# An RWKV block on one core: the recurrence per batch on lanes of a head and a quarter of its key channels

## The chip, the core and the metric

The kernel runs on one core of a Trainium2 chip. The metric is the device time of one execution in microseconds (us), and it is given as the median of several runs. Everything is fp32. A core has a matrix engine (TensorE, PE in the profile, with its weight loads as PEld), a vector engine (VectorE, DVE), a scalar engine (ScalarE, ACT), a general engine (GpSimd, POOL) and a sync engine (SyncE, SP) that here only issues DMAs. Each engine runs its own instructions strictly in the order in which the program gives them; semaphores order them between engines. SBUF is the on-chip memory of 128 partitions, PSUM the accumulator memory of the matrix engine.

## The reference

There are 32 batches of 128 steps with 512 channels; 32 heads of 16 channels. A layer norm, a token shift and five mixes give the inputs of five projections. Then each head runs a recurrence over the 128 steps with a 16 x 16 state, and a group norm, a gate and two more matrix products follow. Cut to what matters:

```python
xn = _ln(x, ln1_w, ln1_b); sx = _token_shift(xn, state[:, 1])
xxx = tanh((xn + sx * maa_x) @ maa_w1) ... @ maa_w2
x5 = xn[:, :, None] + sx[:, :, None] * (maa_stack + xxx)
w = exp(-exp(time_decay + tanh(x5[:, :, 1] @ decay_w1) @ decay_w2))
r, k, v = x5[..3] @ Wr.T, x5[..0] @ Wk.T, x5[..2] @ Wv.T ; g = silu(x5[..4] @ Wg.T)
def step(s, (r_t, k_t, v_t, w_t)):            # per batch and head, s is 16 x 16
    a = k_t[:, :, :, None] * v_t[:, :, None, :]
    out = einsum('bhk,bhkd->bhd', r_t, u * a + s)
    return (a + w_t[:, :, :, None] * s, out)
att = group_norm(outs) * gn_w + gn_b
x = x + att * g @ Wo.T
xn2 = _ln(x, ln2_w, ln2_b); sx2 = _token_shift(xn2, state[:, 0])
x = x + sigmoid(xr @ ffn_Wr.T) * (square(relu(xk @ ffn_Wk.T)) @ ffn_Wv.T)
```

## The kernel before, in words

**Groups.** The 32 batches go in 8 groups of 4 (`GB`, `NG`), so that a group is 512 columns in the channel layout (128 partitions of channels, four chunks e of them, batch and step along the row). For each group a front (layer norm, mixes, projections: `front_mix`, `front_proj`, `front_gate`), a recurrence (`rec_*`) and a back (`back`) are made. The last group's back is made in two halves of two batches.

**Order.** Nothing is scheduled by the chip. `Plan.run` (lines 147 to 190) keeps a model of the five engines, the buffers and one DMA queue. Every step of the work is an `Op` with an engine and an estimated time. Among the steps that can start about first, the one with the earliest due time (`DUE`) is issued next, and so one fixed order of instructions for each engine comes out, written once.

**Projections.** `matmuls` (line 392) gives four matmuls of 128 x 128 by 512 columns for each output chunk; in the trace each fp32 matmul is two instructions. Two narrower forms put two matmuls side by side in the array: `first_split` (line 398, 64 or 32 output columns each, two column tiles) and `side_by_side` (line 411, 64 rows each, two row tiles).

**Into lanes.** The recurrence works on lanes: one partition for a (batch, head) pair, 4 x 32 = 128 of them, and all 16 key channels along the row. `to_lanes` (lines 414 to 421) copies each output chunk of w, k, v and r from the channel layout to lanes by four DMAs from SBUF to SBUF, two issued by SP and two by ACT, in runs of 512 bytes. That is 64 DMAs for a group.

**Preparation.** Two steps are folded into one, so that the scan runs over 64 pairs. `prep` (line 569) multiplies k at even steps by w at odd ones, r at odd steps by w at even ones (lines 604, 606), and makes the product of decays w01 (line 625). `bonus` (line 632) sums r·k·u over the 16 key channels (lines 635 to 643, one instruction per key channel) and r·k of neighbouring steps (lines 648 to 655). All this runs on VectorE in the lane layout.

**Recurrence.** One unit is (key channel q, half dh of the 8 value channels): 32 units for a group, 256 in all. ACT writes the decays into PSUM (line 680) and the first state (line 691); POOL multiplies k by v (line 705) and adds the pairs (line 709); VectorE scans (line 727) and multiplies by r (line 729) into `rm`. TensorE then sums over q: `rec_pe` (line 762) transposes `rm` against a permuted identity, accumulating in PSUM, 8 transposes for each unit, and 8 more for a 17th unit that VectorE makes for the bonus (lines 736 to 743). ACT copies the sum from PSUM to `y` (line 776).

**Back.** Group norm (lines 804 to 819), transposes back into the channel layout (line 830), scaling, the gate from DRAM (line 834), then Wo (line 850), layer norm, and the feed-forward part (lines 392, 924, 940), and the output.

Of the kernel before, what the change touches and what calls it, by code (L numbers as in the profile page):

```python
# [14 lines left out]
P = 128  # L15
B, L, E = 32, 128, 512
H, S = 32, 16
NE = E // P
HE = P // S
GB = 4  # L20
NG = B // GB
# [4 lines left out]
NU = NDH * (S + 1)  # L26
# [19 lines left out]
EPSILON = 0.0457  # L46


DUE = {"rec": (0.169, 1.075), "mix": (-5.141, -3.246), "proj": (-5.191, 5.259), "gate": (0.565, 0.599), "prep": (-4.508, 1.678), "back": (0.059, 3.118), "last1": (-21.936, 10.98), "warm0": (-5.0, -3.0), "warm1": (5.624, 7.819), "last2": (6.858, 12.052)}
# [23 lines left out]
class Plan:  # L73
# [12 lines left out]
    def add(self, gen, v0, v1, steps):  # L86

        st = [gen, None, 0, v0, (v1 - v0) / steps]
        self.streams.append(st)
        self.advance(st, None)  # L90
# [92 lines left out]
def rwkv6_block(ctx: ExitStack, tc: tile.TileContext, x, prev, s0, vecs, u, maa_w1, maa_w2,  # L183
                decay_w1, decay_w2, wr, wk, wv, wg, wo, fk, fr, fv, out):

# [8 lines left out]
    def tag(pool, shape, name, bufs):  # L203
        def make():
# [8 lines left out]
        (big, [P, S, L], "w", 1), (big, [P, S, L], "r", 2), (big, [P, S, L], "k", 2), (big, [P, S, L], "v", 2),  # L213
        (big, [P, GB * H, S], "y", 1),
        (big, [P, S, T2], "w01", 1), (big, [P, S, S], "st", 2), (big, [P, L], "rk", 2), (big, [P, T2], "a10", 2),
        (big, [P, DH, L], "am", 1), (big, [P, DH, T2], "a", 2), (big, [P, DH, L], "rm", 2),
# [3 lines left out]
        (ps, [P, N], "ps", 4), (ps, [P, DH, T2], "sc", 2), (ps, [P, DH, P], "acc", 1),  # L220
    ]
    plan = Plan({name: tag(pool, shape, name, bufs) for pool, shape, name, bufs in spec})

# [4 lines left out]
    u_sb = const.tile([P, S], F32, name="u_sb")  # L228

# [8 lines left out]
    by_head = const.tile([P, P], F32, name="by_head")  # L240
    make_identity(nc, ident)
    nc.gpsimd.tensor_copy(by_head.rearrange("p (b e h) -> p b e h", b=GB, e=NE),
                          ident.rearrange("p (b h e) -> p b e h", b=GB, e=NE))
    nc.gpsimd.memset(mhalf, -0.5)
    nc.gpsimd.memset(thb.t, 0.0)
    nc.vector.memset(w2p, 0.0)

    def constants():
# [18 lines left out]
        for e in range(NE):  # L267
            nc.sync.dma_start(out=lanes(u_sb, e), in_=u[e * HE : (e + 1) * HE, :].unsqueeze(0).to_broadcast([GB, HE, S]))

    def lanes(t, e):  # L270


        return t[e::NE]
# [10 lines left out]
    def load_x(g, need=None, bs=range(GB)):  # L284
        b0, b1 = bs[0], bs[-1] + 1
        (xt,) = yield Op(SP, 0.4, w=[(0, None)], alloc=["x"], xfer=part(4.5, bs), need=need)
        nc.sync.dma_start(out=xt[:, b0:b1, :], in_=x[g * GB + b0 : g * GB + b1].rearrange("b t e -> t b e"))
        return xt
# [8 lines left out]
    def center(w):  # L297


# [14 lines left out]
        centered.append(dw)  # L314

    def part(us, bs):

        return us if len(bs) == GB else us * len(bs) / GB + 0.03

    def layernorm_T(g, src, sums, vw, vb, which, use, take, need=None, bs=range(GB)):  # L320

        b0, nb_ = bs[0], len(bs)
        bsl, cols = slice(b0, b0 + nb_), slice(b0 * L, (b0 + nb_) * L)
        if sums is None:
            xh = src
            stats, mv = yield Op(DVE, 0.88, r=[(src, b0)], w=[(0, b0), (1, b0)], alloc=["stats", "mv"])
            for b in bs:  # L330
                if b != b0:
                    yield Op(DVE, 0.88, r=[(src, b)], w=[(stats, b), (mv, b)])
                nc.vector.bn_stats(stats[:, b, :], src[:, b, :])
                nc.vector.bn_aggr(mv[:, b, :], stats[:, b, :])
# [21 lines left out]
        for b in bs:  # L356
# [6 lines left out]
                       pv[:, 1 - which, :, g * GB + b0 : g * GB + b0 + nb_])  # L363
        late = []

        def evict(e, pt):
            yield Op(ACT, part(0.78, bs), r=[(pt, None)], w=[(xnT, e)])
            nc.scalar.activation(xnT[:, e * GB + b0 : e * GB + b0 + nb_, 1 : L + 1], bt(pt[:, cols]), AF.Identity,
                                 bias=col(vb, e), scale=col(vw, e))
            yield from use(xnT, e, pt, tiles)  # L370
# [15 lines left out]
    def row(xnT, e, shift, bs=range(GB)):  # L386

        return xnT[:, e * GB + bs[0] : e * GB + bs[-1] + 1, shift : shift + L]

    def matmuls(p, w, xin, e, cols=slice(0, N)):  # L390
        for c in range(NE):
            nc.tensor.matmul(p, lhsT=w[:, c, e * P : (e + 1) * P], rhs=xin[:, c, cols], start=(c == 0), stop=(c == NE - 1))  # L392

    def first_split(p, w, rows, xin):

        for c in range(NE):
            for h in range(2):
                nc.tensor.matmul(p[h * XD : h * XD + rows, 0 : N // 2], lhsT=w[:, c, :],  # L398
                                 rhs=xin[:, c, h * N // 2 : (h + 1) * N // 2], start=(c == 0), stop=(c == NE - 1))

    def in_both_halves(t, p, rows):

        for h in range(2):
            for k in range(2):
                nc.scalar.activation(t[k * XD : k * XD + rows, h * N // 2 : (h + 1) * N // 2],
                                     p[h * XD : h * XD + rows, 0 : N // 2], AF.Tanh)

    def side_by_side(pp, w, up, low):

        for p, h, t in zip(pp, (slice(0, XD), slice(XD, P)), (up, low)):  # L410
            nc.tensor.matmul(p.t, lhsT=w[h, :], rhs=t[h, :], start=True, stop=True)  # L411

    def to_lanes(d, name, src, e):

        for eng, queue, bs, end in ((SP, nc.sync, (0, 1), []), (ACT, nc.scalar, (2, 3), [src])):
            if name not in d:
                (d[name],) = yield Op(eng, 1.32, r=[(src, None)], w=[(0, (e, eng))], alloc=[name], xfer=1.2, end=end)
            else:
                yield Op(eng, 1.32, r=[(src, None)], w=[(d[name], (e, eng))], xfer=1.2, end=end)
            for b in bs:  # L420
                queue.dma_start(out=lanes(d[name].t[b * H : (b + 1) * H], e), in_=src[:, b * L : (b + 1) * L])

    def front_mix(g, d):

# [5 lines left out]
        need = (lambda: "ln2" in data[g - 3]) if g > 2 else None  # L430
        def use(xnT, e, pt, tiles):

            yield Op(ACT, 0.75, w=[(pt, None)])
            nc.scalar.activation(pt.t, pt.t, AF.Identity, bias=col(V_LN1B, e), scale=col(V_LN1W, e))
            sx, xin = tiles
            yield Op(DVE, 0.69, r=[(xnT, e), (xnT, "p"), (pt, None)], w=[(sx, e)])
            nc.vector.tensor_tensor(bt(sx[:, e, :]), row(xnT, e, 0), bt(pt.t), ALU.subtract)
            yield Op(DVE, 0.75, r=[(pt, None), (sx, e)], w=[(xin, e)], end=[pt])
            nc.vector.scalar_tensor_tensor(xin[:, e, :], sx[:, e, :], col(V_MAAX, e), pt.t, ALU.mult, ALU.add)
# [3 lines left out]
        (pm,) = yield Op(PE, 8 * PASS, r=[(xin, None)], w=[(0, None)], alloc=["ps"])  # L443
        for c in range(NE):
            nc.tensor.matmul(pm.t, lhsT=w1_sb[:, c, 0 : 4 * XM], rhs=xin[:, c, :], start=(c == 0), stop=(c == NE - 1))  # L445
        (pm2,) = yield Op(PE, 2 * PAIR, r=[(xin, None)], w=[(0, None)], alloc=["ps"], end=[xin])
        first_split(pm2, w1_sb[:, :, 4 * XM : 5 * XM], XM, xin)
        (tha,) = yield Op(ACT, 0.6, r=[(pm, None)], w=[(0, 0)], alloc=["tha"])
        nc.scalar.activation(tha[:, 0, :], pm.t, AF.Tanh)

        yield Op(ACT, 0.6, r=[(pm, None)], w=[(tha, 1)])
        nc.scalar.activation(tha[0:XD, 1, :], pm[XD:P, :], AF.Tanh)
        yield Op(ACT, 0.6, r=[(pm, None)], w=[(tha, 2)], end=[pm])
        nc.scalar.activation(tha[XD:P, 1, :], pm[0:XD, :], AF.Tanh)
        yield Op(ACT, 1.6, r=[(pm2, None)], w=[(thb, None)], end=[pm2],
                 need=(lambda: "mixed" in data[g - 1]) if g else None)
        in_both_halves(thb, pm2, XM)

        done = [0, 0]

        def mixed(m, i, pp, x5):

            for f, p in zip((2 * i, 2 * i + 1), pp):
                if g and m in ON_POOL:
                    yield Op(DVE, 0.75, r=[(p, None), (sx, None)], w=[(x5, f)], end=[p])
                    nc.vector.scalar_tensor_tensor(x5[:, f, :], p.t, col(V_MAA + m, f), sx[:, f, :], ALU.add, ALU.mult)  # L466
                    yield Op(POOL, 1.08, r=[(xnT, None)], w=[(x5, f)], port=True)
                    nc.gpsimd.tensor_tensor(bt(x5[:, f, :]), bt(x5[:, f, :]), row(xnT, f, 1), ALU.add)  # L468
                else:
                    yield Op(DVE, 0.75, r=[(p, None), (sx, None)], w=[(p, None)])  # L470
                    nc.vector.scalar_tensor_tensor(p.t, p.t, col(V_MAA + m, f), sx[:, f, :], ALU.add, ALU.mult)  # L471
                    yield Op(DVE, 0.69, r=[(p, None), (xnT, None)], w=[(x5, f)], end=[p])
                    nc.vector.tensor_tensor(bt(x5[:, f, :]), bt(p.t), row(xnT, f, 1), ALU.add)  # L473
                done[1] += 1
# [3 lines left out]
        for m in (1, 0, 3, 2, 4) if g else (1, 0, 2, 3, 4):  # L478
            up, low = (thb.t, thb.t) if m == 4 else (tha[:, 0, :], tha[:, 1, :]) if m < 2 else (tha[:, 1, :], tha[:, 0, :])
            for i in range(2):  # L480

                pp = yield Op(PE, PAIR, r=[(thb, None), (tha, None)], w=[(0, None), (1, None)],
# [535 lines left out]
```

## Time and profile before

| | us |
|---|---|
| median of 3 runs (lowest, highest) | 1519.36 (1518.51, 1522.76) |
| span of the profiled execution, first to last instruction | 1519.1 |
| PE busy | 1433.7 |
| DVE busy | 1266.1 |
| POOL busy | 1026.1 |
| ACT busy | 657.3 |
| first scan (line 727) starts | 131.3 |
| last sum of the recurrence copied (line 776) starts | 1435.4 |

The profiled execution's own time is its span; it differs from the median by 0.3 us. "Busy" is the time in which an engine has at least one instruction of its own in flight, so the overlapping tails of short matmuls count in it. A row of the groups names the source line, the engine, the operation, what it writes and reads, the shape and the count, then the busy time of the group and the mean duration of one instruction in ns, then the idle time of the engine ahead of it and what ended that. A row of the timeline merges neighbours of one line: start, length, engine, line, count. A row of the windows gives the busy time of each engine in one stretch, the granted TensorE clock as a share of full speed, and the DMA share. The distance from one group to the next is read from the timeline: the reduce of line 807, one for each group, starts at 475.4, 645.7, 816.1, 986.5 and 1156.9 us, that is, every 170.4 us.

### The profile page before, as it was taken

The page shows a single profiled execution, that of the slowest core. Times are in us where ns is not written, and L with a number is a line of the kernel's source. Part 1 is how long each engine was busy: PE and PEld are TensorE (multiplying, and loading weights), DVE is VectorE, ACT ScalarE, POOL GpSimd, SP SyncE. Part 2 cuts the span into 40 slices and gives each one's busy share as a digit, 9 for nine tenths or more (in the row PEclk, how much of TensorE's full clock was granted, in tenths as well). Part 3 has the DMA queues.
Part 4 walks back from the last instruction along what each step waited for, and adds up shares of the span by engine and source line. Part 5 has one row for each costly group of instructions (what it writes and reads, how often), then busy time and mean ns, then how long its engine had stood idle before and what let it go on. Part 6 is the DMA issues. An engine that isn't in the chain of part 4 may idle for free.

```text
span 1519.1 us, 17193 instructions
## 1 busy us (share of the span) xinstructions
PE 1433.7 (94%) x5644; PEld 775.6 (51%) x5644; DVE 1266.1 (83%) x1618; ACT 657.3 (43%) x1279; POOL 1026.1 (68%) x632
## 2 busy tenths in 40 slices
PE   8997999899999999999999999999999999778998
PEld 7333454455544555455544555455544555454564
DVE  4537789989998899899988899899988888978742
ACT  4333243424743366423843365423833354344252
POOL 3014894877886959687786959687776959778500
PEclk9798999899999999999999999999999999889999
DMA  6120331334304521243304521344314421400220
GB/s 226 45 81 27 109 104 35 108 117 132 111 30 134 182 88 42 88 144 132 112 32 137 182 91 36 95 141 128 111 32 142 150 73 59 160 28 28 83 84 28
DMA packets 127561, 146.91 MB, mean 97 GB/s; under 512 B 8176, under 2 KB 77296, under 8 KB 126448
## 3 DMA queue, kind: packets, MB, share of 16 engines
q1 hardware_dynamic: 92112, 128.81, 25.5%
q10 hardware_dynamic: 35360, 17.02, 3.8%
q8 instruction: 44, 0.72, 0.2%
q14 instruction: 45, 0.37, 0.1%
HBM read 94.41 MB, written 17.83 MB: 74 GB/s over the span
## 4 chain that ended last, share of the span: by engine, by line
PE 50%; DVE 23%; POOL 14%; issue 6%; ACT 4%; DMA 2%; SPq 1%; ACTq 0%; POOLq 0%; DVEq 0%
PE ps L392 17%; POOL am L705 8%; PE acc L762 8%; PE ps L940 6%; PE ps L924 6%; PE ps L411 6%; POOL a L709 5%; DVE sc L727 4%; DVE rm L729 3%; PE ps L850 2%; PE ps L445 2%; DVE ps L635 2%; DMA x<-in_x 2%; PE ps L398 1%; DVE rk L643 1%
## 5 line engine op out<-in xcount | busy, mean ns | idle before, releaser
L705 POOL TENSOR_TENSOR am<-v,k 128x1024 f32<-128x1024 f32 x256 | 610.9, 2386 | 71.1 <-DMA r<-blk 52.7
L392 PE MATMUL ps<-mx,wt 128*128 128x512 f32 (+1 forms) x1312 | 581.3, 591 | 7.7 <-DVE mx L885 3.1
L709 POOL TENSOR_TENSOR a<-am 128x504 f32<-128x504 f32 x256 | 286.6, 1120 | 192.0 <-DVE sc L727 173.2
L392 PEld LDWEIGHTS ps<-mx,wt 128*128 128x128 f32 x1312 | 242.6, 193 | 273.7 <-issue 261.7
L729 DVE TENSOR_TENSOR rm<-sc,r 128x1024 f32<-128x1024 f32 x256 | 312.8, 1222 | 35.3 <-PE acc L762 20.3
L727 DVE TENSOR_TENSOR_SCAN sc<-sc,a 128x512 f32<-128x512 f32 x256 | 313.4, 1224 | 31.5 <-POOL a L709 28.7
L762 PE MATMUL acc<-by_head,rm 128*128 128x128 f32 x2176 | 288.6, 282 | 31.6 <-DVE rm L729 27.8
L762 PEld LDWEIGHTS acc<-by_head,rm 128*128 128x128 f32 x2176 | 250.9, 145 | 130.6 <-issue 56.5
L680 ACT COPY sc<-w 128x512 f32<-128x512 f32 x256 | 151.4, 592 | 230.4 <-DVE rm L729 200.5
L468 POOL TENSOR_TENSOR mx<-mx,xnT 128x512 f32<-128x512 f32 x84 | 99.5, 1196 | 40.0 <-DVE mx L466 39.4
L691 ACT COPY a<-st 128x8 f32<-128x8 f32 x256 | 51.4, 203 | 159.6 <-DVE sc L727 132.4
L924 PE MATMUL ps<-wt,mx 128*128 128x512 f32 x256 | 115.7, 594 | 0.0
L541 ACT COPY blk<-ps 128x512 f32<-128x512 f32 x96 | 56.0, 583 | 133.9 <-PE ps L392 127.4
L850 PE MATMUL ps<-wt,mx 128*128 128x512 f32 x256 | 111.7, 592 | 0.2 <-DVE rk L643 0.2
L353 POOL TENSOR_TENSOR rstd<-rstd,mhalf 128x4 f32<-128x4 f32 (+1 forms) x17 | 20.2, 1191 | 129.0 <-DVE rstd L351 129.0
L411 PE MATMUL ps<-tha,w2p 64*128 64x512 f32 x256 | 91.3, 676 | 14.3 <-DVE mx L473 6.8
L940 PE MATMUL ps<-wt,ev 128*128 128x512 f32 x224 | 101.7, 596 | 2.7 <-DVE mx L473 2.7
L471 DVE SCALAR_TENSOR_TENSOR ps<-ps,vec,sx 128x512 f32<-128x512 f32 x76 | 57.1, 752 | 34.7 <-PE ps L411 34.3
L466 DVE SCALAR_TENSOR_TENSOR mx<-ps,vec,sx 128x512 f32<-128x512 f32 x84 | 61.7, 743 | 22.1 <-PE ps L411 22.1
L850 PEld LDWEIGHTS ps<-wt,mx 128*128 128x128 f32 x256 | 48.2, 190 | 59.8 <-issue 55.0
L924 PEld LDWEIGHTS ps<-wt,mx 128*128 128x128 f32 x256 | 46.4, 190 | 51.1 <-issue 46.9
L940 PEld LDWEIGHTS ps<-wt,ev 128*128 128x128 f32 x224 | 40.5, 190 | 45.3 <-issue 39.7
(111 smaller groups left out, 1406.9 us busy)
## 6 DMA issues: line engine op xcount, KB each, us to landing
x<-in_x SPq DMA_DIRECT2D x15, 1024.0 KB
wt<-in_wk SPq DMA_DIRECT2D x8, 1024.0 KB
wt<-in_wr SPq DMA_DIRECT2D x8, 1024.0 KB
wt<-in_wg SPq DMA_DIRECT2D x8, 1024.0 KB
dgate<-blk SPq DMA_DIRECT2D x32, 256.0 KB
wt<-in_wo SPq DMA_DIRECT2D x8, 1024.0 KB
wt<-in_fk SPq DMA_DIRECT2D x8, 1024.0 KB
wt<-in_fr SPq DMA_DIRECT2D x8, 1024.0 KB
```

The source lines that it names most:

```text
L392: nc.tensor.matmul(p, lhsT=w[:, c, e * P : (e + 1) * P], rhs=xin[:, c, cols], start=(c == 0), stop=(c == NE - 1))
L411: nc.tensor.matmul(p.t, lhsT=w[h, :], rhs=t[h, :], start=True, stop=True)
L468: nc.gpsimd.tensor_tensor(bt(x5[:, f, :]), bt(x5[:, f, :]), row(xnT, f, 1), ALU.add)
L680: nc.scalar.copy(sc.t, d["w01"][:, q : q + 1, :].to_broadcast([P, DH, T2]))
L705: nc.gpsimd.tensor_tensor(am.t, v[:, ds, :], k[:, q : q + 1, :].to_broadcast([P, DH, L]), ALU.mult)
L709: nc.gpsimd.tensor_tensor(a[:, :, 1:T2], am2[:, :, 0 : T2 - 1, 0], am2[:, :, 0 : T2 - 1, 1], ALU.add)
L727: nc.vector.tensor_tensor_scan(scf, scf, a.t.rearrange("p d n -> p (d n)"), 0.0, ALU.mult, ALU.add)
L729: nc.vector.tensor_tensor(pair(rm.t), sc.t.unsqueeze(3).to_broadcast([P, DH, T2, 2]), r2[:, q : q + 1, :, :].to_broadcast([P, DH, T2, 2]), ...
L762: nc.tensor.matmul(acc[:, i, :], lhsT=rm[:, i, :], rhs=by_head, is_transpose=True, start=(q == 0 and i % 4 == 0), stop=(q == S), skip_grou ...
L850: nc.tensor.matmul(p.t, lhsT=att[:, c, b * L : (b + 1) * L], rhs=wot[:, c, :], start=(c == 0), stop=(c == NE - 1))
L924: nc.tensor.matmul(p.t, lhsT=xr[:, c, b * L : (b + 1) * L], rhs=frt[:, c, :], start=(c == 0), stop=(c == NE - 1))
L940: nc.tensor.matmul(p2.t, lhsT=kv[:, c, b * L : (b + 1) * L], rhs=fvt[:, c, :], start=(c == 0), stop=(c == NE - 1))
```

## The change

**Lanes.** A lane is now (head, quarter of the key channels): 32 x 4 = 128 partitions for one batch, with 4 key channels along the row. The recurrence is made batch by batch. A unit is as large as before, and there are 8 for a batch, 256 in all. The order over time is the same scan over 64 pairs.

**Into lanes.** `to_lanes` goes. The pair products are made in the channel layout: `decay` makes w01, `k_out` and `r_out` multiply straight out of PSUM. Each chunk is stored to DRAM (16 stores for a group), and `load_rows` loads it per batch: one DMA each for k, w01 and r, four for v, because each of the four quarters needs all of v, and four for `v2`, which is v with a quarter of the steps per lane, in runs of 128 bytes. All of these are issued by SP; ACT issues none of them.

**Sums.** `rec_pe` no longer transposes. For each key channel q it makes 8 matmuls (two halves, four quarters j of the steps) with a 128 x 32 selection matrix `sel` as weights and 256 columns of `rm` as the moving side. Each writes 32 PSUM partitions, so the four quarters lie in four column tiles of the array.

**Bonus.** The products r·k are made in the channel layout (`r_out`), summed over channels by narrow matmuls (`bonus_sums`), multiplied by v on POOL (`rec_bonus`) and added on VectorE where the sum leaves PSUM (`rec_out`). The 17th unit, `bonus` and `prep` go.

**Back.** The output of the recurrence has lanes of (quarter of the steps, head); 16 DMAs for a group, from SBUF to SBUF, bring it back into channels in place of the transposes. The reduce of the group norm now runs along a stride.

**Groups.** `SIZES` makes 9 groups, of 2, 4, 4, 4, 4, 4, 4, 4 and 2 batches; the back in halves goes. Due times, buffer counts (3 `rm`, 2 `acc`) and the dummy matmuls at the end (`warm1`, which goes) change too.

```diff
-NG = B // GB
+Q = 4
+TC = L // Q
+SIZES = (2, 4, 4, 4, 4, 4, 4, 4, 2)
+NG = len(SIZES)
...
+        (big, [P, Q, T2], "wL", 2), (big, [P, Q, L], "rL", 2), (big, [P, Q, L], "kL", 2), (big, [P, S, L], "vL", 2),
+        (big, [P, S, TC], "v2", 1), (big, [P, S, TC + TC // 2], "bo", 1), (big, [P, GB, TC + TC // 2], "rk", 2),
...
+        def store(name, src, f, width, end):
...
+            nc.sync.dma_start(out=d[name].t[rows, 0:width], in_=t[:, 0:width])
...
+                nc.vector.tensor_tensor(w01[:, 0:nb, 1:T2], w4[:, :, 0 : T2 - 1, 0], w4[:, :, 0 : T2 - 1, 1], ALU.mult)
+                yield from store("dw", w01, f, n // 2, [])
...
+        def k_out(p, f):
...
+            nc.scalar.copy(pk[:, f, cols], p[:, cols])
...
+            nc.scalar.copy(od_(ev[:, cols]), od_(p[:, cols]))
...
+            nc.vector.tensor_tensor(ev_(ev[:, cols]), ev_(p[:, cols]), od_(wch[:, f, cols]), ALU.mult)
+            yield from store("dk", ev, f, n, [ev])
+
+        def r_out(p, f):
...
+            nc.vector.tensor_tensor(od_(ev[:, cols]), od_(p[:, cols]), ev_(wch[:, f, cols]), ALU.mult)
...
+            nc.scalar.copy(ev_(ev[:, cols]), ev_(p[:, cols]))
...
+            nc.vector.tensor_tensor(pa[:, f, 0 : n // 2], od_(p[:, cols]), ev_(pk[:, f, cols]), ALU.mult)
...
+            nc.vector.tensor_tensor(pk[:, f, cols], p[:, cols], pk[:, f, cols], ALU.mult)
+            yield from store("dr", ev, f, n, [ev])
...
+    def bonus_sums(g, d, pk, pa):
...
+                for j in range(Q):
+                    nc.tensor.matmul(p[j * H : (j + 1) * H, o : o + nb * width].rearrange("p (b c) -> p b c", b=nb),
+                                     lhsT=lhs[:, e, :], rhs=tv[:, :, j * width : (j + 1) * width],
...
+    def load_rows(tagname, src, xfer, us):
...
+            if tagname == "vL":
+                rows = sb.t.rearrange("(h s) n -> h s n", s=S)[:, :, b * L : (b + 1) * L]
+                for a in range(Q):
+                    nc.sync.dma_start(out=t.t[a::Q], in_=rows)
+            elif tagname == "v2":
...
+                for j in range(Q):
+                    nc.sync.dma_start(out=t.t[j * H : (j + 1) * H],
+                                      in_=rows[:, :, b * L + j * TC : b * L + (j + 1) * TC])
+            else:
...
+                nc.sync.dma_start(out=t.t, in_=sb.t.rearrange("(l q) n -> l q n", q=Q)[:, :, b * w : (b + 1) * w])
...
-                    for i in range(DH):
-
-                        nc.tensor.matmul(acc[:, i, :], lhsT=rm[:, i, :], rhs=by_head, is_transpose=True,
-                                         start=(q == 0 and i % 4 == 0), stop=(q == S), skip_group_check=True)
...
+                for dh, rm in enumerate(rms):
+                    for j in range(Q):
+                        nc.tensor.matmul(
+                            acc[j * H : (j + 1) * H, dh * DH * TC : (dh + 1) * DH * TC].rearrange("p (d c) -> p d c", c=TC),
+                            lhsT=sel, rhs=rm[:, :, j * TC : (j + 1) * TC], start=(q == 0 and dh == 0), stop=(q == Q - 1), skip_group_check=True)
...
+    def rec_bonus():
...
+            nc.gpsimd.tensor_tensor(one, v2.t, rk[:, b : b + 1, 0:TC].to_broadcast([P, S, TC]), ALU.mult)
...
+            nc.gpsimd.tensor_tensor(odd, odd, two, ALU.add)
...
+    def rec_out():
...
+            nc.vector.tensor_tensor(y[:, :, b, :], acc.t.rearrange("p (s c) -> p s c", c=TC), bo[:, :, 0:TC], ALU.add)
...
+            for j in range(Q):
+                nc.sync.dma_start(out=yc[:, e, j * nb * TC : (j + 1) * nb * TC],
+                                  in_=yv[j * H + e * HE : j * H + (e + 1) * HE])
```

## The prediction, on record before the change ran

> **What bounds the kernel now.** I read the page's busy times first, then the windows of the middle, then the timeline of PE there, then the groups by form. The profiled execution's span is 1519.1 us, 0.3 below the median of the runs, so I make the sum against 1519.1.
>
> ```profile
> PE 1433.7 (94%) x5644; PEld 775.6 (51%) x5644; DVE 1266.1 (83%) x1618; ACT 657.3 (43%) x1279; POOL 1026.1 (68%) x632
> ```
> ```profile
> 646.00:806.00 160.00, 157.50 (x621) 83.49 (x621) 147.76 (x187) 74.91 (x149) 119.73 (x73) 1.00 0.31 102
> 806.00:966.00 160.00, 158.04 (x634) 84.23 (x633) 147.79 (x187) 76.62 (x149) 126.90 (x77) 1.00 0.33 109
> ```
>
> The columns of a window are its length and the busy us of PE, PEld, DVE, ACT and POOL, then the granted clock, the DMA share and GB/s. In the middle PE is busy 98.4% of the time at full clock; DVE 92.4%, POOL 77%. So PE sets the pace of 170.4 us a group, with DVE close behind. At the ends PE is not the limit: the first scan starts at 131 us, and after the last sum, at 1435, come 84 us of back.
>
> What the sums over key channels cost is read from the timeline of PE, by the distance between starts, because busy times count overlapping tails:
>
> ```profile
> 722.79 1.04 PE L762 MATMUL acc<-by_head,rm 128*128 128x128 f32 x8
> 723.66 3.60 PE L392 MATMUL ps<-mx,wt 128*128 128x512 f32 x8
> ...
> 762.52 3.60 PE L445 MATMUL ps<-mx,w_sb 128*128 128x512 f32 x8
> 766.05 1.92 PE L398 MATMUL ps<-mx,w_sb 128*32 128x256 f32 x16
> 767.91 1.97 PE L762 MATMUL acc<-by_head,rm 128*128 128x128 f32 x16
> ```
>
> Eight transposes, one unit, take 723.66 - 722.79 = 0.87 us. The row of 128*32 holds 16 instructions in two column tiles.
>
> **PE.** Removed: 272 units x 0.87 = 236.6 us, and the 128 transposes of y (line 830) at 0.109, 14.0. Added: for each of 128 (batch, key channel) pairs 16 instructions of 256 columns in four column tiles. No row has four tiles; the nearest has two. There 512 columns take 3.53 / 8 = 0.44 us with the entry (L445 to L398), 0.43 without (eight of L392 from 723.66 to the next start at 727.10), so 256 columns take 0.213 to 0.215. Sixteen in a row would be 3.41 us; the row took 767.91 - 766.05 = 1.86, which is 8 x 0.213 = 1.71 and 0.15 over. So two tiles run fully side by side. With four it is 4 x 0.213 = 0.85, and I put 0.2 for the two changes of form: 1.05 us. The bounds are 0.85 and 3.41 + 0.2 = 3.6 (nothing side by side); I take 1.05, the value nearest to the row, which had no loss. 128 x 1.05 = 134.4. That the second instruction of an fp32 matmul does not block the next tile is in these lines, at half clock:
>
> ```profile
> 50.23 1.22 PE L411 MATMUL ps<-tha,w2p 64*128 64x512 f32 x1 [0.64 <-DVE mx L473]
> 50.23 1.22 PE L411 MATMUL ps<-blk,dw2p 64*128 64x512 f32 x1
> 51.24 1.06 PE L411 MATMUL ps<-tha,w2p 64*128 64x512 f32 x1
> 51.25 2.76 PE L411 MATMUL ps<-blk,dw2p 64*128 64x512 f32 x3
> ```
>
> Two matmuls in different tiles start together, and so do their second instructions, 1.02 us later. The bonus sums add, for a group of four, 64 instructions in four tiles, 8 steps of 128 columns and 8 of 64: 8 x 0.107 + 8 x 0.053 + 0.2 = 1.5 us, 12 in all. PE in all: -236.6 - 14.0 + 134.4 + 12 = -104 us, 13.0 for each of 8 groups' worth. From 98.4% of 170.4 = 167.7 us PE falls to 154.7.
>
> The Trainium skill speaks against this: "TensorE: Matmul & The Clock Gate", Measured speedup vs the span model, gives three column tiles a gain of 2.38 and not 3, 0.79 of the full gain; by that, 0.85 would be 1.07 us, 128 x 0.22 = 28 us more, and the time some 1440. Its section The mechanism says that matmuls start strictly in program order. If that held a tile back until the second pass of the one before, the sum would be that of my first rival; the rows at 50.23 say otherwise for two row tiles, and no run here shows four column tiles.
>
> **DVE.** Removed, whole groups with all their forms:
>
> ```profile
> L643 DVE SCALAR_TENSOR_TENSOR rk<-ps,u_sb,rk 128x128 f32<-128x128 f32 x120 | 42.0, 350 | 3.7
> L635 DVE TENSOR_TENSOR ps<-r,k 128x512 f32<-128x512 f32 x32 | 33.6, 1052 | 0.1
> L736 DVE TENSOR_TENSOR rm<-v,rk 128x1024 f32<-128x1024 f32 x16 | 25.4, 1588 | 0.0
> L739 DVE TENSOR_TENSOR ps<-v,a 128x512 f32<-128x512 f32 x16 | 20.5, 1278 | 1.6 <-ACT blk L514 1.4
> L651 DVE TENSOR_REDUCE a<-blk 128x64 f32<-128x512 f32 x8 | 8.4, 1046 | 0.2
> ```
>
> These five make 129.9 us; lines 583, 591, 604, 606, 624, 625, 640, 648, 654, 655 and 743 make another 67.4, in all 197.3. Added, for each of 4 chunks of a group: four instructions of 256 columns (w01, k, two for r) at 0.42, the row of L841 for 256, and one of 512 at 0.69; 9.5 us a group, 76 in all. Those that step by two in PSUM have no row; bounds 0.42 and 0.69, and I take 0.42, since the doubled steps of L604 in SBUF cost nothing (1.219 for 1024). `rec_out` is 32 x 0.69 = 22. The group norm's reduce runs along a stride: L651 does so at 2.04 ns an element, L807 without at 1.11, so up to 2048 x 0.93 = 1.9 us x 8 = 15 (bounds 0 and 15; I take 15). DVE in all: -197 + 113 = -84, per group 157.4 - 10.5 = 147.
>
> **POOL** gets the bonus product: 512 and 256 and 256 elements for a batch, 1.2 + 0.6 + 0.6 by L468 (1196 ns for 512): 2.4 x 32 = 77 us, from 131 to 141 a group. **ACT** loses the copies of line 776 (31 us) and 256 DMA issues, gains small copies (12 us); at 43% it hides both ways.
>
> **DMA and SP.** The 64 copies into lanes of a group go, half from SP's queue, half from ACT's. SP issues instead 11 loads for a batch, and for a group 16 stores and 16 DMAs of y, at 0.61 (median of L421) or 0.34 (L566): 44 x 0.61 + 16 x 0.34 + 16 x 0.61 = 42 us of a group, some 52 with the weights, gates, x and outputs that it issues now. That is a third of SP's time, and SP has no other work; what it hides behind is the two-deep buffering of k, w, r and v. The packets: ACT's queue shows 35,360 in 3.8% of 16 engines' span, 0.026 us each. The loads make 3,072 of 512 bytes, 512 of 256 and 2,048 of 128 for a batch, 180,000 in all; at no more than 0.026 each, 293 us of 16 engines, or 21% of the span, where the copies of now take twice 3.8%. The DMA share of 0.31 to 0.33 would stay under 0.5. So DMA is hidden as long as the loads run a batch, about 40 us, ahead.
>
> **Waits that are added.** The 16 DMAs of y wait on SP for the end of the group norm, and behind them on SP stand loads for the next batch and stores of the next front; the batch under way has its rows already, so a wait under some 30 us reaches nobody. On PE the 16 matmuls wait for both halves of a key channel; behind them stand projections whose results are needed tens of us later, and DVE goes on into the third `rm` buffer, 3.7 us (scan, multiply, scan), longer than one projection step of 3.43: at nothing, as the 20 us of DVE's waits for PE now. If that cover is gone, each of the 256 units can lose about 1 us.
>
> **The sum.** With PE at 98.4% of the time a group would take 157.2 us; DVE would then be at 93.5% and POOL at 90%. Three engines so near their limit meet more often, so I take 97%: 159.5 us, 10.9 less than now, 8 x 10.9 = 87 us. At the end two batches instead of four are left: 55 us of PE's work in the 84 becomes 27, but the 16 DMAs of y put 10 us of issue ahead of it where transposes took 4: I take 20 us off (bounds 5 and 30). At the start half a front comes before the first scan, but the half that is saved is made later, and the way through DRAM is longer: 0 (bounds -20 and +20). 1519.1 - 87 - 20 = 1412.
>
> **Rivals.** (1) **The four tiles run only two at a time.** 1.71 + 0.2 = 1.91 us, 128 x 0.86 = 110 us more: 1522, between 1500 and 1535. For it: no row with four. Against it: two tiles lose nothing. Nothing side by side, 3.6 us, would be 1740; the L398 row speaks against it, and I count it with the slower cases. (2) **PE is relieved, and DVE and POOL waiting on each other keep the pace.** DVE already waits 28.7 us for POOL's L709 in the scans; at a pace of 165 to 170 us the time is 1412 + 8 x 5.5 = 1456 and more, 1450 to 1500. Against it: near the end (1400 to 1430) units follow each other at 3.53 us on POOL with nothing between, 113 a group, so POOL has room. (3) **Slower: SP holds the loads.** SP issues in order. `v2` and `bo` have one buffer each; a `v2` load waits for POOL's bonus of the batch before, which waits for `bo`, which `rec_out` frees after the last sum of the batch before that. If k, w or r of the next batch stands behind that wait, each batch starts late: 0.7 (`rec_out`) + 2.4 (POOL) + 4 x 0.61 + 0.61 = 6.2 us and the landing; 32 x 6.2 = 198, time 1610. It decides from (87 + 20) / 32 = 3.3 us a batch on. Against it: k, w, r and v have two buffers, so their loads may go a batch early. The change does what it says in any case; the tiles are the part that might not.
>
> **How the numbers follow.** Forecast, 1372 to 1450: 0.61. Below 1372 (PE stays at 98.4% and the start shortens by 20 or more): 0.04. Rival 2: 0.10. Rival 1: 0.10, of which 0.03 is faster, 0.03 within, 0.04 slower. Rival 3 with all that is slower: 0.15. Within 0.3%, 4.6 us, a measurement of this kernel can't tell a change. Faster 0.61 + 0.04 + 0.10 + 0.03 = 0.78, same 0.03, slower 0.19. The range from 1372 to 1535 leaves out 0.04 and 0.15.
>
> **What would show it.** The new row of 16 matmuls 128*32 by 256 columns: 1.0 to 1.1 us to the next start (right), 1.9 or 3.6 (wrong). A distance of 158 to 161 us between groups; DVE about 1180 us, POOL about 1105 busy; the scan waiting for no DMA. POOL or the scan's chain waiting for loads would show rival 3. Most likely wrong: the ends, and POOL's waits.

## The result and the profile after

The changed kernel takes 1527.42 us (median of 20 runs, 1523.12 to 1535.79), the kernel before beside it 1520.26 (20 runs). The ratio is 1.0044, 95% interval 1.003 to 1.0057: slower by 7 us, or 0.4%, where 107 us less was forecast. The profiled execution's span is 1522.0. Its busy times are:

```profile
PE 1333.5 (88%) x6060; PEld 606.3 (40%) x6060; DVE 1198.4 (79%) x1600; ACT 633.7 (42%) x1358; POOL 1084.2 (71%) x747
```

PE has 100 us less to do and DVE 68 less, POOL 58 more. So the work went away as planned, and yet the span grew: PE now stands idle for 188.5 us of it instead of 85.4, DVE for 323.6 instead of 253.0 (span less busy time). Where this happens is seen by cutting both spans at the first and at the last scan:

| us | to the first scan | first to last scan | after the last scan | span |
|---|---|---|---|---|
| before | 131.3 | 1295.3 | 92.5 | 1519.1 |
| forecast (87 off the middle, 20 off the end) | 131.3 | 1208 | 72.5 | 1412 |
| after | 88.5 | 1317.1 | 116.4 | 1522.0 |
| after, with two mends shown below | 88.7 | 1280.5 | 95.8 | 1465.0 |

The start gained 43 us that were not forecast; the recurrence and the end lost them again. The same cut finer, as the us for each 32 units of the recurrence (the last entry has 31 distances):

| | | | | | | | | |
|---|---|---|---|---|---|---|---|---|
| before | 166.5 | 164.8 | 170.4 | 170.4 | 170.4 | 170.4 | 157.4 | 125.0 |
| after | 190.5 | 159.6 | 181.5 | 168.4 | 169.8 | 154.8 | 160.9 | 131.5 |
| two mends | 190.3 | 153.6 | 175.3 | 163.3 | 166.4 | 149.9 | 156.3 | 125.3 |

The first 32 units take 24 us longer after the change, so about half of what the start gained is given back there. POOL's timeline shows one reason, in front of the second group's first unit: its rows of v are not there yet. SP's timeline, below it, shows the last two of the four stores of this v to DRAM just ahead of that. The first group, of two batches, is over before the second group's front is.

```profile
180.51 2.36 POOL L723 TENSOR_TENSOR am<-vL,kL 128x1024 f32<-128x1024 f32 x1 [16.50 <-DMA vL<-dv]
```
```profile
166.63 4.95 SPq L524 DMA_DIRECT2D dv<-blk  x2
```

With the two mends this wait is still there, 16.99 us.

Three windows of the kernel after (us, then busy PE, PEld, DVE, ACT, POOL, granted clock, DMA share, GB/s):

```profile
88.50:279.00 190.50, 169.88 (x763) 69.25 (x764) 165.81 (x214) 72.23 (x163) 148.21 (x103) 0.93 0.48 148
788.50:958.40 169.90, 163.51 (x713) 70.20 (x714) 145.25 (x188) 78.94 (x167) 139.34 (x93) 0.97 0.54 161
1405.60:1522.00 116.40, 82.11 (x216) 39.09 (x216) 29.71 (x58) 35.16 (x63) 1.72 (x2) 0.85 0.20 64
```

and the end of the kernel before:

```profile
1426.60:1519.00 92.40, 83.29 (x346) 52.67 (x344) 36.86 (x83) 34.84 (x71) 1.40 (x2) 0.98 0.23 74
```

In the middle of the kernel after PE is busy 96% of the time, but at a granted clock of 0.97, where it was 1.00 before; at the end the clock is 0.85 (0.98 before), and PE has nearly as much to do there as before, 82.1 us for 83.3. Now look at the column tiles, in PE's timeline:

```profile
1335.32 1.07 PE L761 MATMUL acc<-rm,sel 128*32 128x256 f32 x16
1336.32 3.70 PE L938 MATMUL ps<-wt,ev 128*128 128x512 f32 x8
```

From start to next start 16 instructions in four column tiles take 1.00 us, where the prediction had 0.85 for four that run side by side without any loss and 1.91 for two at a time. So four run side by side, and my first rival is out; that the time fell into its interval, 1500 to 1535, is chance.

Two places lose time that no part of the forecast has. **The way of y back into channels.** The sync engine's timeline, then DVE's and PE's in the same microseconds:

```profile
891.94 3.62 SPq L835 DMA_DIRECT2D ev<-y  x4
...
896.90 5.13 SPq L835 DMA_DIRECT2D ev<-y  x4
...
902.69 4.53 SPq L835 DMA_DIRECT2D ev<-y  x4
...
908.43 4.27 SPq L835 DMA_DIRECT2D ev<-y  x4
912.74 0.52 SPq L841 DMA_DIRECT2D blk<-dgate  x1
```
```profile
917.78 0.69 DVE L790 TENSOR_TENSOR y<-acc,bo 128x512 f32<-128x512 f32 x1 [5.04 <-DMA ev<-y]
```
```profile
922.04 2.73 PE L424 MATMUL ps<-thb,w2p 64*128 64x512 f32 x4 [6.10 <-DVE mx L850]
924.70 1.93 PE L761 MATMUL acc<-rm,sel 128*32 128x256 f32 x16
926.74 11.38 PE L857 MATMUL ps<-wt,mx 128*128 128x512 f32 x24
```

The 16 DMAs, with a few stores of the next front between them, keep SP's queue for 21 us, where I had put 10. DVE's next write into y waits for them to have read it, 5.04 us, and the gate's product (L850) comes late behind that; PE stands for 6.10 us. Then the 16 matmuls that took 1.00 us take 2.04: PE runs at half clock for some 10 us (granted clock 0.50 from 918.2 to 928.4). The Trainium skill, "TensorE: Matmul & The Clock Gate", HAM oscillation, asks for no idle gap of PE above some 3.4 us; this row agrees with it.

The same comes in six of the nine groups: L790 waits 4.9 to 6.6 us, and PE stands for 6.1 to 9.6 us just behind. The view names `ev<-y` for two of these six waits and other DMAs for four; in the two runs below that take the 16 DMAs away, `y_by_copy` and `y_dram`, none of the six is left.

**The end.** DVE's timeline, then ACT's:

```profile
1457.63 0.69 DVE L930 SCALAR_TENSOR_TENSOR x<-ps,x 128x512 f32<-128x512 f32 x1
1458.24 1.85 DVE L815 TENSOR_REDUCE th<-ev 128x64 f32<-128x1024 f32 x1
```
```profile
1456.84 1.06 ACT L812 ACTIVATE ev<-y 128x1024 f32<-128x1024 f32 x1 [2.84 <-PE ps L938]
```

The last sum of the recurrence was ready at 1410, but the reduce of the last group norm starts at 1458, after the last output of the group before (L930). Its input, the squares (L812), needs a buffer `ev`, of which there is one, and the group before keeps it for `kk` until its last matmul (L938). From 1409 to 1457 us PE itself works on the feed-forward part of that group of four.

### The profile page after: what moved, and what is told of

Read it like the earlier page. It is cut to its first block, busy times and chain, and to the rows that moved or that the text cites. A ratio compares the mean times of both kernels' runs of the same rounds, so it can differ in the third digit from the quotient of the medians.

```text
span 1522.0 us, 18535 instructions
## 1 busy us (share of the span) xinstructions
PE 1333.5 (88%) x6060; PEld 606.3 (40%) x6060; DVE 1198.4 (79%) x1600; ACT 633.7 (42%) x1358; POOL 1084.2 (71%) x747
## 3 DMA queue, kind: packets, MB, share of 16 engines
q1 hardware_dynamic: 291424, 221.10, 48.8%
## 4 chain that ended last, share of the span: by engine, by line
PE 58%; DVE 16%; issue 9%; SPq 6%; POOL 4%; DMA 4%; ACT 2%; POOLq 0%; DVEq 0%; ACTq 0%
PE ps L407 26%; PE ps L923 6%; PE ps L938 6%; PE ps L857 5%; PE acc L761 5%; SPq L835 4%; PE ps L424 4%; DVE sc L742 3%; DVE rm L744 3%; POOL am L723 2%; PE ps L413 2%; PE ps L394 1%; PE ps L450 1%; DVE mx L470 1%; DVE th L815 1%
## 5 line engine op out<-in xcount | busy, mean ns | idle before, releaser
L723 POOL TENSOR_TENSOR am<-vL,kL 128x1024 f32<-128x1024 f32 x256 | 604.0, 2360 | 70.9 <-DMA vL<-dv 53.2
L407 PEld LDWEIGHTS ps<-mx,wt 128*128 128x128 f32 x1440 | 268.2, 193 | 304.8 <-issue 240.5
L727 POOL TENSOR_TENSOR a<-am 128x504 f32<-128x504 f32 x256 | 263.3, 1028 | 102.9 <-DVE sc L742 88.5
L744 DVE TENSOR_TENSOR rm<-sc,rL 128x1024 f32<-128x1024 f32 x256 | 312.2, 1219 | 14.4 <-PE acc L761 4.4
L700 ACT COPY sc<-wL 128x512 f32<-128x512 f32 x256 | 150.8, 589 | 257.6 <-DVE rm L744 250.7
L761 PE MATMUL acc<-rm,sel 128*32 128x256 f32 x2048 | 152.5, 408 | 61.5 <-DVE rm L744 61.4
L472 POOL TENSOR_TENSOR mx<-mx,xnT 128x512 f32<-128x512 f32 (+1 forms) x96 | 105.2, 1113 | 68.6 <-DVE mx L470 68.1
L761 PEld LDWEIGHTS acc<-rm,sel 128*32 128x32 f32 x2048 | 54.4, 112 | 171.6 <-DVE rm L744 82.4
L938 PE MATMUL ps<-wt,ev 128*128 128x512 f32 x256 | 117.6, 602 | 0.3 <-DVE mx L477 0.3
L424 PE MATMUL ps<-tha,w2p 64*128 64x512 f32 (+1 forms) x288 | 86.5, 624 | 10.0 <-DVE blk L644 4.3
L475 DVE SCALAR_TENSOR_TENSOR ps<-ps,vec,sx 128x512 f32<-128x512 f32 (+1 forms) x84 | 55.6, 662 | 23.6 <-PE ps L424 23.3
L938 PEld LDWEIGHTS ps<-wt,ev 128*128 128x128 f32 x256 | 46.7, 190 | 62.7 <-issue 50.7
L470 DVE SCALAR_TENSOR_TENSOR mx<-ps,vec,sx 128x512 f32<-128x512 f32 (+1 forms) x96 | 65.5, 706 | 5.7 <-PE ps L424 5.7
```

Source lines behind the costliest of these rows:

```text
L407: nc.tensor.matmul(p[:, cols], lhsT=w[:, c, e * P : (e + 1) * P], rhs=xin[:, c, cols], start=(c == 0), stop=(c == NE - 1))
L424: nc.tensor.matmul(p[:, cols], lhsT=w[h, :], rhs=t[h, cols], start=True, stop=True)
L472: nc.gpsimd.tensor_tensor(bt(x5[:, f, cols]), bt(x5[:, f, cols]), row(xnT, f, 1, nb), ALU.add)
L700: nc.scalar.copy(sc.t, w[:, q : q + 1, :].to_broadcast([P, DH, T2]))
L723: nc.gpsimd.tensor_tensor(am.t, v[:, ds, :], k[:, q : q + 1, :].to_broadcast([P, DH, L]), ALU.mult)
L727: nc.gpsimd.tensor_tensor(a[:, :, 1:T2], am2[:, :, 0 : T2 - 1, 0], am2[:, :, 0 : T2 - 1, 1], ALU.add)
```

## The experiments

All are written against the kernel after, if nothing else is said; each ratio is to the kernel before.

**y's way.** `y_by_copy` replaces the 16 DMAs by copies on ACT:

```diff
-            for j in range(Q):
-                nc.sync.dma_start(out=yc[:, e, j * nb * TC : (j + 1) * nb * TC],
-                                  in_=yv[j * H + e * HE : j * H + (e + 1) * HE])
+            nc.scalar.copy(yc[:, e, cols].rearrange("p (j m) -> p j m", j=Q), yv[:, e * Q : (e + 1) * Q, :])
```

> The changed kernel, with the 16 DMAs per group that bring y back into channels replaced by four ACT copies of the same size; the channels are not put back in order, so this part of the computation is left out. The order of all other instructions is the same. Theory A (the long way of y, 29 us from the group norm's last multiply to the gate's first multiply, holds PE about 6.5 us in each group and 14 us at the end, and each hold costs some 4 us more at half clock): about 1455, between 1435 and 1475. Theory B (VectorE and TensorE are both so full that a stall taken away comes back as another): 1500 or more, mostly the 14 us of the end.

Measured: 1477.8 us, 0.9728 (0.9701 to 0.9756), 50 us less than after. Its fourth to sixth stretches of 32 units fall to 163.3, 166.4 and 149.9, the same as in the last line of the table. `y_dram` keeps the computation whole: one store of y to DRAM and four loads.

```diff
+            if e == 0:
+                dy = dram.tile([P, S, GB * TC], F32, tag="dy", bufs=2, name=f"dy_{g}")
+                nc.sync.dma_start(out=dy[:, :, 0 : nb * TC], in_=yv)
+            nc.sync.dma_start(out=yc[:, e, cols].rearrange("p (j m) -> p j m", j=Q),
+                              in_=dy.rearrange("(j h) s m -> (h s) j m", j=Q)[e * P : (e + 1) * P, :, 0 : nb * TC])
```

> The changed kernel, complete, with y brought back into channels by way of DRAM: one store of the whole y and four loads for a group in place of 16 DMAs from SBUF to SBUF, at the same place in the same order of instructions. SP issues 5 DMAs for a group (some 4 us) where the 16 took 15 to 21, and one more landing is waited for. Theory A (the 16 issues on SP make the way of y long, and that way holds TensorE and VectorE): most of the 50 us that the copies on ACT gave back, 1480 to 1500. Rival (it is the landing of the DMAs, or their low rate, and not the issuing): the second landing makes it no better, 1520 to 1535.

Measured: 1487.01, 0.9785 (0.9771 to 0.98). So 40 of the 115 us between forecast and result lie in the 16 DMAs. The number of packets is not what cost it: on SP's queue `y_dram` has 295,984 for 291,424 in the kernel after. Whether it was the issue of 16 DMAs on SP or the slowness of the transfers themselves is not separated, since both versions change both.

**The end.** `kk_in_pk` gives `kk` of the last two groups another buffer, `pk`:

```diff
-                    (kk,) = yield Op(ACT, part(0.6, nb), r=[(p, None)], w=[(0, f)], alloc=["ev"], end=[p])
+                    (kk,) = yield Op(ACT, part(0.6, nb), r=[(p, None)], w=[(0, f)], alloc=["pk" if g >= NG - 2 else "ev"], end=[p])
```

> The changed kernel, with the feed-forward activations of the last two groups kept in the buffer pk, which no front needs any more by then, and not in the single buffer ev; nothing is left out. The order of instructions is written anew. Theory of the end (the last group's back cannot begin before the back of the group before it has released ev, 1409 to 1457 us): 20 to 45 us off, 1482 to 1507. Rival (the way of y and the chain through the last back are the length of the end): within 8 us of 1527.

Measured: 1507.94, 0.9926 (0.9902 to 0.9951), 19 us less than after. The planner wrote the order anew for this edit, so buffer and order change together. `y_dram_kk` has both mends:

> The changed kernel, complete, with both edits: y by way of DRAM and the activations of the last two groups in pk. If the two losses (the way of y; the one buffer ev at the end) are separate, their gains add up: 1527 - 19 - 30 to 40 = 1468 to 1480, below the kernel before. If they are the same loss seen twice: about 1490 to 1500.

Measured: 1468.59, 0.9671 (0.9655 to 0.9687). The two add up (40 + 19 = 59). This complete kernel takes 52 us less than the kernel before, about half of the 107 that were forecast, and is still 57 us above the forecast.

**Does PE set the pace?** `before_half_sums` leaves out every second key channel's transposes in the kernel before (`range(DH if q % 2 == 0 else 0)`), 128 x 0.87 = 111 us of PE. `quarter_sums` leaves out three quarters of the new sums in the kernel after (`enumerate(rms if q == 0 else ())`, with `start` and `stop` to match), 96 us.

> The kernel before, with the transposes of odd key channels left out (half of the sum is left out): 1024 of 2176 go, 128 x 0.87 = 111 us of TensorE's time, in the same order. If TensorE alone set the pace before the change, as the prediction took it: 111 x 0.9 off, about 1420. If VectorE, at 92% busy, stands right behind it: about 8 x 6 us off, 1460 to 1490. If the written order holds the pace whatever TensorE does: above 1505.

> The changed kernel, with the summing matmuls made for the first of the four key channels of a lane alone (three quarters of the sum are left out): 1536 of 2048 matmul instructions go, 96 x 1.0 us of TensorE's time, in the same order of instructions. If TensorE still sets the pace after the change: about 1527 - 85 = 1440. If it no longer does (VectorE, POOL and the waits written into the order do): 1505 to 1525.

Measured: 1494.45, 0.9832 (0.9818 to 0.9847), and 1508.94, 0.9925 (0.9902 to 0.9948). 111 us less on PE brought 26 us, 96 us brought 18. The premise of the forecast falls, and already for the kernel before (in its written order; no other order of it was tried). In its middle, without half of the sums, a window of 168 us:

```profile
628.00:796.00 168.00, 158.00 (x547) 76.36 (x546) 158.45 (x200) 81.50 (x159) 131.78 (x79) 1.00 0.33 109
```

PE could have finished 14 us earlier than in 170.4; the four middle stretches of 32 units take 165.9 to 167.1, with DVE at 94%.

**Which engines share the pace?** Starting from `y_dram_kk` and always in its written order, three cuts were tried in all combinations: PE as in `quarter_sums`; DVE, half of the multiply by r; POOL, half of the product of k and v, the last two for three of four key channels.

```diff
+                    h = T2 if q == 0 else T2 // 2
-                        pair(rm.t), sc.t.unsqueeze(3).to_broadcast([P, DH, T2, 2]),
+                        pair(rm.t)[:, :, 0:h, :], sc[:, :, 0:h].unsqueeze(3).to_broadcast([P, DH, h, 2]),
...
+                    h = L if q == 0 else L // 2
-                    nc.gpsimd.tensor_tensor(am.t, v[:, ds, :], k[:, q : q + 1, :].to_broadcast([P, DH, L]), ALU.mult)
+                    nc.gpsimd.tensor_tensor(am[:, :, 0:h], v[:, ds, 0:h], k[:, q : q + 1, 0:h].to_broadcast([P, DH, h]), ALU.mult)
```

> The kernel with both mends (y by one store and four loads through DRAM, kk of the last groups under its own tag), 0.967 of before, with three quarters of the recurrence's 16-matmul sums left out: only the first quarter of the key channels is summed, 128 rows of 16 become 32, 96 us of PE less; the written order stays. Theory A, PE's pace: 8 groups lose some 11 us each, time about 1380, ratio 0.91. Theory B, PE and DVE meet so often in the written order that neither alone sets the pace: 15 to 30 us less, 1440 to 1455, ratio 0.95 to 0.957. Theory C, DVE alone: the same time, 0.967.

> The kernel with both mends, with half of DVE's multiply by r left out for the last three quarters of the key channels (64 of 128 positions; the matmuls read the written half twice, so their number and shape stay): 192 multiplies of 1.22 us become some 0.62, 115 us of DVE less; the written order stays. Theory A, PE's pace: the same time, ratio 0.967. Theory B, both together: 15 to 40 us less, ratio 0.94 to 0.957. Theory C, DVE's pace: over 80 us less, ratio under 0.915.

> Both cuts at once: three quarters of the sums left out and half of the multiply left out for the last three quarters of the key channels; 96 us of PE and 115 us of DVE less, the written order stays. Theory A (PE alone): as the kernel with the sums left out. Theory B (two engines that meet): much more than the two cuts give one by one, 80 us or more off, ratio under 0.915. Rival D, the written order with its waits between engines or a third engine (POOL, 74% busy) holds the pace: hardly more than the sum of the two cuts, ratio 0.92 to 0.95.

> The kernel with both mends, 0.967 of before, with half of POOL's product k times v left out for the last three quarters of the key channels (64 of 128 positions; the pair sums that follow read the written half twice, in two instructions): some 190 to 220 us of POOL less, the written order stays. If POOL is the third engine that the others meet: 10 to 40 us less, ratio 0.94 to 0.96. If the written order alone holds the pace: the same time, 0.967.

> All three cuts at once: three quarters of the sums, half of the multiply by r and half of the product k times v left out for the last three quarters of the key channels; the kernel with the first two cuts took 0.949 of before. If POOL was what the other two waited for: over 60 us less than that, ratio under 0.91. If the written order holds the pace, with each engine's instructions queued behind another stage's: 0.93 to 0.949, though no engine is then busy more than 87% of the time.

> The kernel with both mends and half of the multiply by r and half of the product k times v left out for the last three quarters of the key channels; all sums over the channels stay, so PE has its full work. If PE's cut is worth its size once the two others have room: this takes 50 to 75 us more than with all three cuts, 1434 to 1459, ratio 0.943 to 0.96. If PE hardly matters: under 1410, ratio under 0.928.

> The kernel with both mends and three quarters of the sums and half of the product k times v left out for the last three quarters of the key channels; DVE has its full work. If POOL alone stands in PE's way: within 15 us of all three cuts, under 1400, ratio under 0.921. If DVE does too: 1405 to 1435, 0.925 to 0.944.

| cut | us | ratio (95%) | off `y_dram_kk` |
|---|---|---|---|
| PE | 1455.59 | 0.9563 (0.9531 to 0.9595) | 13 |
| DVE | 1457.65 | 0.9585 (0.9561 to 0.9608) | 11 |
| POOL | 1444.58 | 0.9489 (0.9458 to 0.952) | 24 |
| PE, DVE | 1443.55 | 0.9488 (0.946 to 0.9516) | 25 |
| DVE, POOL | 1432.51 | 0.9421 (0.9407 to 0.9435) | 36 |
| PE, POOL | 1406.06 | 0.9255 (0.924 to 0.9271) | 63 |
| all | 1383.9 | 0.909 (0.9055 to 0.9126) | 85 |

The last column is the difference of the medians. By the ratios, each to the kernel before beside it, the differences are up to 4 us larger. The cuts are not of one size: in busy time POOL's takes 180 us (1083.5 to 903.9), DVE's 98 (1198.7 to 1100.8), PE's 75 (1324.5 to 1249.2).

PE's cut of 96 us is worth 13 alone, 14 beside DVE's (1457.65 - 1443.55), 38 beside POOL's (1444.58 - 1406.06) and 49 beside both (1432.51 - 1383.9). So it is above all POOL that holds PE's freed time, though POOL is busy only 74% of the span. DVE stands in the way as well: beside the two others its cut is worth 22 us (1406.06 - 1383.9). My theory that PE and DVE together would give 80 us missed; the pair that comes nearest, with 63, has POOL in it. The waits in the middle show the turn: DVE's scan waiting for POOL, first in `y_dram_kk` (608 to 1087 us), where four other waits of DVE are longer, then in the kernel with PE and DVE cut (755 to 1068 us), where it is the longest, as us in total, times, longest:

```profile
DVE sc L742 <- POOL a L727: 4.3, 8, 1.0
```
```profile
DVE sc L742 <- POOL a L727: 14.1, 14, 2.2
```

With all cuts PE is again near full in the middle, 286.85 of 298 us, at 149 us a group, where the same two stretches of `y_dram_kk` (166.4 and 149.9) have 158:

```profile
725.00:1023.00 298.00, 286.85 (x1003) 124.25 (x1002) 257.08 (x365) 148.16 (x314) 223.81 (x230) 0.99 0.58 180
```

**Or is it the order?** `y_plan` is `y_dram_kk` with the planner's prices set to the trace (for w01 0.85, the reduce 3.7, y's transfers 1.4 and 0.7) and new due times; `y_pe_plan` the same with PE's cut and due times for it.

> The complete kernel with both mends (0.967 of before) with the planner's prices set to the times of the trace (y's store and loads, w01 0.85, the group norm's reduce 3.7) and new due times for its steps. If the order was what kept the freed time of PE from use: 30 us less or more, ratio under 0.948. If the engines meet in any order: within 15 us of the kernel with both mends, 0.957 to 0.977.

> The same with three quarters of the sums left out (only the first quarter of the key channels is summed), the planner told that they cost nothing, and due times laid out anew for that. In the old order this cut gave 0.956. If the order holds back PE's freed time: under 0.925. If DVE and POOL keep the pace in any order: 0.945 to 0.965.

Measured: 1463.87, 0.963 (0.9604 to 0.9655), and 1450.3, 0.9526 (0.9498 to 0.9554). The new order takes about 5 us off each, and PE's cut is worth 14 us again. Two orders can't exclude a third, but the order was not simply stale. `y_plan` is the fastest complete kernel run, though its interval meets that of `y_dram_kk`.

Some results lie in none of the ranges that I gave: `y_by_copy`, `kk_in_pk`, `y_pe`, `y_dve` and `y_dve_pool` by at most 3 us, `before_half_sums` between two of them.

## Why the prediction was wrong

- **"So PE sets the pace"**: wrong, and the first step that failed. A busy share of 98.4% showed that PE was full, not that the others could go faster: 111 us less of PE in the kernel before brought 26. The sum put the 10.9 us on all 8 groups; the table shows that only four of the eight stretches of before ran at 170 us. With both mends these four have 163.7 on average (175.3, 163.3, 166.4, 149.9) for the 159.5 of the sum, and the last two hardly change (156.3 and 125.3, 157.4 and 125.0 before). Against the forecast's middle of 1208 us, after has 109 too many. 37 of them go with the mends (1317.1 - 1280.5); of the other 72, some 17 lie in these four stretches, 21 in the last two, and 35 in the first, 24 of which are the start's gain coming back and no matter of PE's pace.
- **"a wait under some 30 us reaches nobody"**, for the 16 DMAs of y: put at nothing, and the second step that failed, with 40 us by `y_dram`. In the group shown the DMAs take 17.6 us of SP, 21 with what lies between (over the run 0.604 to 2.091 each, median 0.701, where I took 0.61), and the wait reached DVE and PE in six groups. I had looked for who waits on SP behind them, not for who waits to write y.
- **Rival 2**, DVE and POOL keeping the pace at 1456 and more, came nearest to the mechanism, and its interval, 1450 to 1500, holds the time with both mends; that of the kernel after lies outside. I had it at 0.10, because of a stretch near the end where POOL had room. That stretch has no front beside it; the middle does.
- **The end, 20 us off**: 24 us on instead. `ev` accounts for 20.6 of the 44 us between: with `kk` in `pk` the end falls from 116.4 to 95.8, with y by way of DRAM alone only to 112.4. For the other 23, the sum took half of PE's work off, 55 us to 27, and this did not happen: with both mends PE still has 80.7 us to do after the last scan, where before had 83.3, because the group of four ahead of the last one is not done either. No run tried to shorten that.
- **The start, 0**: 43 us earlier, within no bound that I gave; 24 of them come back in the first 32 units (190.3 with the mends for 166.5).
- **The column tiles, 1.05 us**: right, 1.00. **PE -104**: right, -100. **DVE -84**: -68; the reduce along a stride took 3.70 us for 2.28, 1.4 more, where I put 1.9, but the 28 full instructions of w01 averaged 0.89 for 0.42, 13 us more in all. **POOL 1105**: 1084. **DMA share under 0.5**: 0.44 to 0.54 over the eight stretches, a little more than put. POOL's product (L723) waits for a load twice only, before the first unit and at the second group, and no scan does; rival 3 did not come.

## What to carry to other kernels

A full engine is the limit only if the others have room in the same stretch: before pricing a relief, take the work out of the kernel before (here one line, 111 us of PE) and see what the time does; it gave 26 us. A saving per group holds for the groups that run at that pace, not for all. When a transfer takes the place of an engine's work, look for who waits to write what it reads, and for how many buffers the next stage needs.

## What the runs showed of the hardware

Four column tiles of fp32 lose little: 16 instructions of 256 columns in 1.00 us, where one by one they would be 3.41 by the prediction's rows, a gain of 3.4, 0.85 of the full one. The Trainium skill, "TensorE: Matmul & The Clock Gate", Measured speedup vs the span model, has 2.38 for three column tiles, 0.79 of the full gain.

A DVE instruction from SBUF to SBUF can stand still while POOL works. The two w01 instructions (L543, 252 elements, median 0.41 us each) here take 3.03 us, and end just after POOL's product that began beside them:

```profile
534.07 3.03 DVE L543 TENSOR_TENSOR w<-wch 128x252 f32<-128x252 f32 x2
534.42 2.40 POOL L723 TENSOR_TENSOR am<-vL,kL 128x1024 f32<-128x1024 f32 x1
```

Of the 36 instructions of L543, 13 start while POOL's product (L723) runs; each of them ends 0.15 to 0.28 us after that product does. Those of 252 elements that start while POOL is idle take 0.40 to 0.41. In the busy time this counts as work of DVE, and no view of waits names it. POOL's cut shows it too: `y_dram_kk`, first, and `y_pool` have the same 1600 instructions of DVE, and with the shorter products DVE is busy for 32 us less.

```profile
PE 1324.5 (90%) x6060; PEld 602.1 (41%) x6060; DVE 1198.7 (82%) x1600; ACT 632.9 (43%) x1358; POOL 1083.5 (74%) x747
```
```profile
PE 1322.7 (92%) x6060; PEld 604.3 (42%) x6060; DVE 1167.1 (81%) x1600; ACT 632.8 (44%) x1358; POOL 903.9 (63%) x939
```

How much of the 24 us that POOL's cut gave comes from this, no run here separates.
